# Two attention layers and two expert layers in one kernel: the shared stretch issued in traced order, later stages in small pieces

## The chip, the cores and the metric

The kernel runs on one core of one Trainium2 chip. The metric is the device time of one execution in microseconds; the time shown is the median of three runs. All arithmetic named here is fp32 unless a type is given.

The engines are named as in the profile: PE does matmuls (its weight loads, PEld, overlap them), DVE and ACT work on 128 partitions of vectors, POOL here adds the two halves of a rope and issues gathers, SP issues the other transfers. Each engine has its own queue of instructions[...].

## The reference, cut to what matters

The input is 2048 tokens of 128 channels. Two layers, each an attention and an expert network, every part with a layernorm before it and a residual after it:

```python
x = x + attn0(ln(x))     # 16 heads of 64, all 2048 x 2048 scores, softmax, rope on q and k,
                         # q, k and v from latents of 64
x = x + ffn0(ln(x))      # 16 experts, 4 a token out of the best 2 of 4 groups of experts:
                         # y += (silu(x@W1+b1) * (x@W3+b3)) @ W2 * weight
x = x + attn1(ln(x))     # 8 heads, sparse: I = sum_h idx_w[h] * relu(q_i[h] . k_i)
                         # local 64 keys kept, later keys masked, top 96 of I taken,
                         # their latents gathered, softmax over the 96, weighted sum
x = x + ffn1(ln(x))      # shared expert of width 256, and 2 of 8 experts of width 128 by the
                         # token's position: exact gelu
```

`attn0` needs all keys before any token's output. After it, a token's way through `ffn0` is its own; `attn1` reads the tokens before it; `ffn1` is its own again.

## The kernel before, in words

The kernel is one class, `Program`. `prologue` loads the weights and computes the latents and the tables. `run` then goes through the first attention in 32 **units**: unit u is a pair of heads `pr` (8 of them) and a group `g` of 512 queries (4 of them), all eight pairs of group 0 first. A unit takes four **steps** s, and a step has two **halves**. Three things are under way in every half, for units that lie some steps apart:

- `by_query` (L265 to L282), for unit u: the scores of 128 queries by 512 keys, for both heads: matmuls into two banks `pa` (L275), the negated maximum `mx` on DVE (L280), and `junk` on ACT (L282), an exponential of which only the row sum is kept. This yields maximum and sum of the softmax.
- `by_key` (L316 to L329), for the unit five steps behind (`BEHIND`): the scores again, transposed, into two banks `pb` (L323), the maxima added by a bf16 matmul with `onesb` (L325), and the exponential `e` on ACT (L329).
- `mean` (L331 to L343), one step later: `e` times the latents `ckv` into `po` (L338). After sixteen of them `o<-po` (L343) takes the result out: once a unit.

Once a unit come `rope` (L235; DVE products `t_q` at L254, their sum `q` on POOL at L255; the keys' `kst` go to DRAM as `kd`), `close` (the sums and the maxima), `turn` (L305, transposes of the maxima, evicted as `mrow`) and `project` (L347, the output product `pp`, added to `xr` on DVE). `keys_of` (L263) loads `ka` and `kb` for the step after next from `kd`.

PSUM is cut into a pool `ps` of five banks (`pa`, `pb`, `rope`), one bank for `po`, and a pool `px` of two banks, from which `x()` gives one to everything else, `turn` and `project` included.

**The later stages.** When a group's eight units are through, `follow(g)` starts: a generator that runs `experts0`, `attention1` and `experts1` for its 512 tokens. Each traces a portion of instructions and then yields an estimate of its microseconds. In the halves of the next group's units `advance(us)` pulls such portions until it has spent `us` times `PACE[g]`: after each `by_key` (1.0), after each `by_query` (1.0) and after the two `mean` (2.0), 6 us of pace a half. If a stream isn't at its end when the next begins, its rest is traced at once. Group 3 has no units after it but the last drain steps, so nearly all of its stream is traced after the loop.

- `experts0` (L518): layernorm, the gate with its ranks (`below`), then for each of 16 experts `hidden` (`p1` and `p3` matmuls, `th` and `z` on ACT, `h` on DVE) and, one expert behind, `py` and its four additions to `xr`. Expert weights `wx` are loaded two ahead.
- `attention1` (L634): keys and index keys of the group, then for each tile n of 128 tokens `index_scores` (L701, matmuls `pi`, `rl` on ACT, sums `v` on DVE), `choose` (L733, four rounds of maximum, index and replacement over `v`, whose length grows with n; then `ixT`), 32 gathers `kv<-table` (L756, indirect transfers that POOL issues), `queries` (L772) and, one tile behind, `attend` (L813: rotation `rgc`/`rgs` of the gathered keys, transposes `ptr`, scores `pl`, `mx`, `e`, transposes `pte`, `po1`, `pj`). The order is index_scores(n), choose(n), attend(n-1), queries(n). `pay` issues one gather or more at each yield, while there are any.
- `experts1` (L925): layernorm, ten expert weights `wd`, two shared experts, the eight by position, the sum and the store of the output.

**The order on the queues.** The program is traced in the order above, and then a scheduler orders each engine's queue: it gives each instruction a priority by its place in the trace, moved ahead by `URGENT` = 500 for those within `high_priority`, and lets an instruction pass earlier ones that can't run yet. `keep_in_program_order` pins the gathers and the first two operations of a rotation. The tile framework puts in the semaphores in either case.

Of the kernel before, what the change touches and what calls it, by code (L numbers as in the profile page):

```python
# [16 lines left out]
P = 128  # L17
# [20 lines left out]
URGENT = 500  # L38
PACE = (1.0, 1.1, 1.2, 1.2)
# [24 lines left out]
def layernorm(nc, pool, src, dst, tag):  # L64

    nt = src.shape[1]
    st = pool.tile([P, nt, 6], F32, tag=tag + "st", name=tag + "st")
    mv = pool.tile([P, nt, 2], F32, tag=tag + "mv", name=tag + "mv")
    for n in range(nt):
        nc.vector.bn_stats(st[:, n, :], src[:, n, :])  # L70
        nc.vector.bn_aggr(mv[:, n, :], st[:, n, :])
    v = pool.tile([P, nt], F32, tag=tag + "v", name=tag + "v")
    nc.vector.tensor_scalar(v, mv[:, :, 1], EPS, None, ALU.add)
    r = rsqrt(nc, pool, v, tag)
    for n in range(nt):
        nc.vector.tensor_scalar(
            dst[:, n, :], src[:, n, :], mv[:, n, 0:1], r[:, n : n + 1], ALU.subtract, ALU.mult
        )


def softplus(nc, pool, out, src, one, tag):

    a = pool.tile(list(out.shape), F32, tag=tag + "a", name=tag + "a", bufs=1)
    nc.scalar.activation(a, src, AF.Abs)
    nc.scalar.activation(a, a, AF.Exp, scale=-1.0)
    nc.scalar.activation(a, a, AF.Ln, bias=one)
    nc.vector.scalar_tensor_tensor(out, src, 0.0, a, ALU.max, ALU.add)


def rotate(nc, eng, pool, out1, out2, mu, cos, sin, tag, bufs=None, keep=None):  # L90

    shape = list(mu.shape)
    c = pool.tile(shape, F32, tag=tag + "c", name=tag + "c", bufs=bufs)
    s = pool.tile(shape, F32, tag=tag + "s", name=tag + "s", bufs=bufs)
    first = eng.tensor_tensor(c, mu, bcast(cos, 2, 2), ALU.mult)
    if keep is not None:
        keep(first)
    second = eng.tensor_tensor(s, mu, bcast(sin, 2, 2), ALU.mult)
    if keep is not None:
        keep(second)  # L100
    eng.tensor_tensor(out1, c[:, :, 0, :], s[:, :, 1, :], ALU.subtract)
    eng.tensor_tensor(out2, s[:, :, 0, :], c[:, :, 1, :], ALU.add)


class Program:
# [23 lines left out]
    def bank(self, name):  # L129

        return self.ps_s.tile([P, 512], F32, tag="ps", name=name)
# [5 lines left out]
    def transposed(self, src, dst, name):  # L137

        pt = self.x(name)
        for j in range(4):  # L140
            self.nc.tensor.transpose(pt[:, j, :], src[:, j, :], self.ident)
        self.nc.scalar.copy(dst, pt.rearrange("p a b -> p (a b)"))

    def prologue(self):
# [40 lines left out]
        for g in range(4):  # L187
            cols = slice(512 * g, 512 * g + 512)
            xn = pp.tile([P, 4, C], F32, tag="xn", name=f"xn{g}", bufs=2)
            layernorm(nc, pp, self.xr[g], xn, "ln0")  # L190
            nc.gpsimd.tensor_tensor(self.xr[g], self.xr[g], xn, ALU.add)
            hn = pp.tile([P, 4, C], F32, tag="hn", name=f"hn{g}", bufs=2)
            layernorm(nc, pp, xn, hn, "ln0")
# [33 lines left out]
        self.ep = self.ctx.enter_context(tc.tile_pool(name="a_e", bufs=7))  # L227
# [37 lines left out]
    def by_query(self, u, i):  # L265
# [11 lines left out]
        with self.tc.high_priority(URGENT):  # L277
            for h in range(2):
                at = (slice(None), qt, kc, slice(h, h + 1))
                nc.vector.tensor_reduce(mx[at], ps[h], axis=AX.X, op=ALU.max, negate=True)  # L280
                junk = self.am.tile([P, 512], BF16, tag="junk", name=f"junk{u}_{i}_{h}")
                nc.scalar.activation(junk, ps[h], AF.Exp, bias=mx[at], accum_out=su[at])  # L282
# [22 lines left out]
    def turn(self, u):  # L305

        nc = self.nc
        pm = self.x(f"pt{u}", dtype=BF16)
# [7 lines left out]
    def by_key(self, u, kb):  # L316
# [10 lines left out]
        with self.tc.high_priority(URGENT):  # L327
            for h in range(2):
                nc.scalar.activation(e[:, h, :], ps[h], AF.Exp)  # L329
# [17 lines left out]
    def project(self, u, h):  # L347
# [4 lines left out]
        pm = self.x(f"pp{u}_{h}")  # L352
# [8 lines left out]
    def run(self):  # L361
# [26 lines left out]
        for s in range(4 * NU + BEHIND + 5):  # L388
            u, j = divmod(s, 4)
            ub, jb = divmod(s - BEHIND, 4)  # L390
            um, jm = divmod(s - BEHIND - 1, 4)
            if u < NU and j == 0 and u + 1 < NU:
                self.rope(self.UNITS[u + 1][0], "q", self.UNITS[u + 1][1])
            if u + 1 < 8:
                self.rope(u + 1, "k", j)
            if s == 4 * 8:
                self.keys.close()
            if s + 2 < 4 * NU:
                self.keys_of((s + 2) // 4, (s + 2) % 4, "a")
            sb = s + 2 - BEHIND  # L400
            if 0 <= sb < 4 * NU:
                self.keys_of(sb // 4, sb % 4, "b")
            for half in range(2):
                pair = range(2 * half, 2 * half + 2)
                for i in pair:
                    if 0 <= ub < NU:
                        self.by_key(ub, 4 * jb + i)
                    advance(1.0)
                    if u < NU:
                        self.by_query(u, 4 * j + i)  # L410
                    advance(1.0)
                if half == 1 and u < NU and j == 3:
                    self.close(u)
                for i in pair:
                    if 0 <= um < NU:
                        self.mean(um, 4 * jm + i)
                if half == 0 and j == 0 and 0 <= u - 1 < NU:
                    self.turn(u - 1)
                advance(2.0)
                if jm == 1 and 0 <= um - 1 < NU:  # L420
                    self.project(um - 1, half)
            if jm == 1 and 0 <= um - 1 < NU:
                self.outs.pop(um - 1)
                if um % 8 == 0:
                    if stream is not None:
                        for _ in stream:
                            pass
                    stream, owed, pace = self.follow(um // 8 - 1), 0.0, PACE[um // 8 - 1]
        if stream is not None:
            for _ in stream:  # L430
                pass
# [86 lines left out]
    def experts0(self, sc, g):  # L518
# [6 lines left out]
        layernorm(nc, sm, xr, xn, "ln1")  # L525
        yield 5.0
        xT = sm.tile([P, 512], F32, tag="xT", name=f"xT1_{g}")
        self.transposed(xn, xT, f"pt1_{g}")
        yield 2.0
# [4 lines left out]
        for j in range(4):  # L534
            nc.tensor.matmul(pg[:, j, :], xT[:, j * P : j * P + P], w["wg"], start=True, stop=True)
        s = sm.tile([P, 4, NE0], F32, tag="s", name=f"gs{g}")
# [4 lines left out]
        yield 2.0  # L541
# [3 lines left out]
        def below(v, n, first, k, tag):  # L545
# [3 lines left out]
            eq = sm.tile(shape, F32, tag="eq", name=f"eq{tag}{g}")  # L549
            nc.vector.tensor_tensor(gt, bcast(v, 2, n), bcast(v, 3, n), ALU.is_gt)  # L550
            nc.vector.tensor_tensor(eq, bcast(v, 2, n), bcast(v, 3, n), ALU.is_equal)
            ff = bcast(first.rearrange("p a b -> p (a b)"), 1, 4)
            e2 = eq.rearrange("p t a b -> p t (a b)")
            nc.vector.tensor_tensor(e2, e2, ff, ALU.mult)
            nc.vector.tensor_tensor(gt, gt, eq, ALU.add)
            rank = sm.tile([P, 4, n], F32, tag="rank" + tag, name=f"rank{tag}{g}")
            nc.vector.tensor_reduce(rank, gt, axis=AX.X, op=ALU.add)
            nc.vector.tensor_scalar(rank, rank, float(k) - 0.5, None, ALU.is_lt)
            return rank
# [4 lines left out]
        gsel = below(gm, NG0, w["first4"], 2, "g")  # L564
        yield 3.0
# [6 lines left out]
        esel = below(ms, NE0, w["first16"], 4, "e")  # L572
        yield 7.0
# [13 lines left out]
        yield 2.0  # L587

        pt = self.x(f"ptw{g}", [P, P])
        nc.tensor.transpose(pt, we.rearrange("p a b -> p (a b)"), self.ident)  # L590
        wt = sm.tile([P, P], F32, tag="wt", name=f"wt{g}")
        nc.scalar.copy(wt, pt)
        yield 1.0
        pb = self.x(f"pb2_{g}")
        nc.tensor.matmul(pb.rearrange("p a b -> p (a b)"), wt, w["b2"], start=True, stop=True)
        nc.vector.tensor_tensor(xr, xr, pb, ALU.add)
        yield 1.5


        hs = {}  # L600
        for e in range(NE0 + 1):
            if e < NE0:
                if e + 2 < NE0:
                    wx.append(self.weights(wp, e + 2, f"wb{g}_{e + 2}"))
                hs[e] = self.hidden(hp, wx[e], xT, w["b13"][:, 0, e : e + 1], self.hb[:, e : e + 1], w["b13"][:, 1, e : e + 1], f"b{g}_{e}")
                yield 2.0
            if e > 0:
                h = hs.pop(e - 1)
                py = self.x(f"py{g}_{e}")
                for j in range(4):  # L610
                    nc.tensor.matmul(py[:, j, :], h[:, j * P : j * P + P], wx[e - 1][:, 2, :], start=True, stop=True)
                yield 1.0
                for j in range(4):
                    nc.vector.scalar_tensor_tensor(
                        xr[:, j, :], py[:, j, :], wh[:, j, e - 1 : e], xr[:, j, :], ALU.mult, ALU.add
                    )
                yield 1.0

    def hidden(self, pool, wx, xT, b1, hb1, b3, name):

        nc = self.nc
        p1, p3 = self.x("p1" + name, [P, 512]), self.x("p3" + name, [P, 512])
        nc.tensor.matmul(p1, wx[:, 0, :], xT, start=True, stop=True)  # L623
        nc.tensor.matmul(p3, wx[:, 1, :], xT, start=True, stop=True)  # L624
# [4 lines left out]
        h = pool.tile([P, 512], F32, tag="h", name="h" + name)  # L629
# [486 lines left out]
```

## Time and profile before

| | us |
|---|---|
| Median of the runs shown (3) | 3028.55 |
| Lowest and highest of them | 3015.8 and 3028.8 |
| Profiled execution | 3467.66 |
| Its span, first to last instruction | 3465.9 |
| Busy in it: PE / ACT / DVE / POOL | 2798.2 / 1739.4 / 1715.1 / 577.9 |
| Last `o<-po` (end of the 32nd unit) | 2900.0 |
| Mean granted PE clock | 0.861 |

The profiled execution is 14.5% longer than the median; durations in the text come from it. A matmul's end is modelled in it, so a busy PE need not be a PE at its peak. The 24 units that share their time with later stages lie between 595 and 2900 us, the stages of group 3 between 2900 and 3466.

### The profile page before, as it was taken

Reading aid. Unit: us, or ns where it says so; the run is one execution under the profiler, and the core shown is the slowest. Engines: PE = TensorE matmul, PEld = TensorE weight load, DVE = VectorE, ACT = ScalarE, POOL = GpSimd, SP = SyncE. Lnnn points to the kernel's source line nnn. Section 1 sums busy time; section 2 is a strip of 40 time slices with the busy share of each in tenths; the row PEclk is TensorE's granted clock in tenths of the full one; section 3 lists DMA queues with packets and bytes.
Section 4 is the critical chain, followed back from the end, with each engine's and each line's share of the span. In section 5 each row is a group of like instructions: output and inputs, shape, how many; then the busy total and the mean of one; then the engine's idle time right before and its main releaser. Section 6 shows DMA issues by size and latency. Waiting matters only on the chain. (4 is left out here: it accounts for less than half of the span.)

```text
span 3465.9 us, 38526 instructions
## 1 busy us (share of the span) xinstructions
PE 2798.2 (81%) x13452; PEld 1256.3 (36%) x13452; DVE 1715.1 (49%) x3749; ACT 1739.4 (50%) x4157; POOL 577.9 (17%) x586
## 2 busy tenths in 40 slices
PE   5999999998788899997697899997696877733426
PEld 3444444343233344442243344342242333312214
DVE  7645444565343444665363545555354624664242
ACT  2766667565464566564464466564363542312213
POOL 1111100002313210002312300002303210061330
PEclk7999999999797799998897899997797978856556
DMA  4211111111111111111111111111111101010000
GB/s 130 64 52 52 59 49 38 37 45 33 34 37 27 31 52 38 41 39 28 32 39 28 30 49 43 39 35 28 31 29 25 23 12 42 24 21 5 14 12 26
DMA packets 98097, 127.74 MB, mean 37 GB/s; under 512 B 31344, under 2 KB 49776, under 8 KB 97904
## 3 DMA queue, kind: packets, MB, share of 16 engines
q1 hardware_dynamic: 81520, 108.48, 11.1%
q0 software_dynamic: 16384, 16.81, 2.4%
q8 instruction: 106, 1.74, 0.2%
q14 instruction: 87, 0.71, 0.1%
HBM read 115.26 MB, written 9.96 MB: 36 GB/s over the span
## 5 line engine op out<-in xcount | busy, mean ns | idle before, releaser
L280 DVE TENSOR_REDUCE mx<-pa 128x1 f32<-128x512 f32 x1024 | 673.2, 686 | 695.7 <-PE pa L275 502.3
L282 ACT ACTIVATE junk<-pa,mx 128x512 bf16<-128x512 f32 x1024 | 699.9, 691 | 423.2 <-DVE mx L280 384.5
L275 PE MATMUL pa<-ka,q 64*128 64x512 f32 x2048 | 777.8, 639 | 87.7 <-ACT junk L282 68.2
L329 ACT ACTIVATE e<-pb 128x512 f32<-128x512 f32 x1024 | 556.5, 597 | 473.2 <-PE pb L325 356.2
L323 PE MATMUL pb<-q,kb 64*128 64x512 f32 x2048 | 693.4, 646 | 99.6 <-ACT e L329 73.1
L756 POOL DMA_INDIRECT kv<-table,ixT x512 | 491.0, 959 | 926.1 <-issue 484.2
L338 PE MATMUL po<-e,ckv 128*64 128x512 f32 x2048 | 552.0, 659 | 1.7 <-issue 1.7
L275 PEld LDWEIGHTS pa<-ka,q 64*128 64x128 f32 x2048 | 272.5, 193 | 351.7 <-ACT junk L282 190.3
L323 PEld LDWEIGHTS pb<-q,kb 64*128 64x128 f32 x2048 | 233.7, 193 | 350.9 <-issue 165.6
L255 POOL TENSOR_TENSOR q<-t_q 128x512 f32<-128x512 f32 x32 | 40.7, 1273 | 1560.7 <-DVE t_q L254 1560.7
L325 PE MATMUL pb<-mrow,onesb 64*128 64x512 bf16 x1024 | 262.8, 386 | 2.0 <-issue 1.9
L338 PEld LDWEIGHTS po<-e,ckv 128*64 128x64 f32 x2048 | 133.9, 146 | 348.9 <-issue 337.3
L282 ACT ACTIVATION_READ_ACCUMULATOR junk<-pa,mx 128x1 f32 x1024 | 209.2, 204 | 0.0
L861 DVE TENSOR_REDUCE mx<-pl 128x2 f32<-128x416 f32 x64 | 37.8, 591 | 343.7 <-remote 158.0
L865 ACT ACTIVATE e<-pl,mx 128x208 f32<-128x208 f32 x128 | 54.4, 431 | 242.6 <-DVE mx L862 173.7
L711 PE MATMUL pi<-kiT,qiT 64*128 64x512 f32 (+4 forms) x320 | 123.9, 632 | 47.3 <-issue 17.9
L831 PE MATMUL ptr<-ident,kv 128*128 128x128 f32 x256 | 44.3, 315 | 94.7 <-issue 66.9
L855 PE MATMUL pl<-kr,qT 64*32 64x128 f32 x1024 | 66.9, 320 | 63.6 <-issue 63.5
L325 PEld LDWEIGHTS <-onesb 64*128 64x128 bf16 x1024 | 75.6, 96 | 112.2 <-issue 90.3
L717 DVE SCALAR_TENSOR_TENSOR v<-rl,iw_sb,v 128x512 f32<-128x512 f32 (+4 forms) x120 | 77.1, 644 | 71.9 <-ACT rl L716 64.2
L832 ACT COPY kr<-ptr 128x512 f32<-128x512 f32 x64 | 37.0, 590 | 142.7 <-PE ptr L831 97.0
L630 DVE SCALAR_TENSOR_TENSOR hb<-thb,zb 128x512 f32<-128x512 f32 x64 | 44.3, 692 | 129.4 <-ACT zb L628 127.4
(266 smaller groups left out, 2856.4 us busy)
## 6 DMA issues: line engine op xcount, KB each, us to landing
ka<-kd SPq DMA_DIRECT2D x128, 256.0 KB
kb<-kd SPq DMA_DIRECT2D x128, 256.0 KB
wb<-in_wx SPq DMA_DIRECT2D x64, 192.0 KB
kd<-kst SPq DMA_DIRECT2D x32, 256.0 KB
kv<-table,ixT POOLq DMA_INDIRECT x512
wd<-in_wx SPq DMA_DIRECT2D x40, 192.0 KB
csk<-in_cs SPq DMA_DIRECT2D x4, 512.0 KB
csq<-in_cs SPq DMA_DIRECT2D x4, 512.0 KB
```

What stands on the lines that cost most here:

```text
L275: nc.tensor.matmul(ps[h], q[rows, qt * P : qt * P + P], k[rows, :], start=True, stop=True)
L280: nc.vector.tensor_reduce(mx[at], ps[h], axis=AX.X, op=ALU.max, negate=True)
L282: nc.scalar.activation(junk, ps[h], AF.Exp, bias=mx[at], accum_out=su[at])
L323: nc.tensor.matmul(ps[h], k[rows, c], q[rows, :], start=True, stop=False)
L325: nc.tensor.matmul(ps[h], self.onesb[rows, :], mrow[rows, :], start=False, stop=True)
L329: nc.scalar.activation(e[:, h, :], ps[h], AF.Exp)
L338: nc.tensor.matmul(self.pos[u][cols, :], self.ckv[:, kb, :], e[:, h, :], start=(kb == 0), stop=(kb == NT - 1))
L711: nc.tensor.matmul(pi[:, : hi - lo], qiT[h // 2][rows, q], kiT[rows, lo:hi], start=True, stop=True)
L717: nc.vector.scalar_tensor_tensor(v[:, lo:hi], rl[:, : hi - lo], w["iw"][:, h : h + 1], v[:, lo:hi], ALU.mult, ALU.add)
L756: nc.gpsimd.indirect_dma_start(out=kv[:, 2 * (g % 16) + g // 16, :], out_offset=None, in_=table[0 : P * (n + 1), :], in_offset=bass.Indire ...
L855: nc.tensor.matmul(pl[32 * j : 32 * j + 32, c, 80:NK], qs[rows, 32 * gr : 32 * gr + 32], kr[rows, gr % 16, :], start=False, stop=(c == 1),)
L865: nc.scalar.activation(e[:, i, :], pl[:, c, :], AF.Exp, scale=SCALE1, bias=mx[:, i : i + 1], accum_out=su[:, i : i + 1],)
```

## The change

Four things are changed.

1. The loop of `run` stands inside `tc.manual_schedule()`: there the scheduler leaves each engine's instructions in traced order, on every queue. `URGENT`, its two `high_priority` blocks and the pins of gathers and rotations are gone; the pin of the table preload stays for group 3, whose stream is traced after the loop and is still ordered by the scheduler.
2. The stages are cut into small pieces, about one engine's portion of a chain each, some 450 a group. `layernorm`, `softplus`, `rotate`, `transposed`, `hidden` and `index_scores` become generators. `merge` alternates pieces of choose(n) with pieces of attend(n-1), which came one after the other before. `paced` issues one gather a piece, in `queries`, the next `index_scores` and in what remains after it; during `attend` there are none. An expert's order is now `p1`, then `th` and `z` with `py` of the expert before, then `p3` with the additions of the expert before, then `h` twice.
3. `advance` runs after each of the two `mean` (1.0 each) instead of once after both (2.0). `PACE` is smaller, as are the estimates in the yields.
4. `turn` and `project` take their banks from `ps` instead of `px`; the pool of `e` has eight buffers instead of seven, and `rl` three instead of two. `e*ri` is done in two halves, and the two Gelus of `experts1` stand together.

The number and size of matmuls, transfers and gathers stay as they are. The diff, cut to its core:

```diff
-URGENT = 500
-PACE = (1.0, 1.1, 1.2, 1.2)
+PACE = (0.86, 0.93, 1.0, 1.0)
...
+def merge(*parts):
+    parts = list(parts)
+    while parts:
+        for p in list(parts):
+            us = next(p, None)
+            if us is None:
+                parts.remove(p)
+            else:
+                yield us
...
-        self.ep = self.ctx.enter_context(tc.tile_pool(name="a_e", bufs=7))
+        self.ep = self.ctx.enter_context(tc.tile_pool(name="a_e", bufs=8))
...
-        with self.tc.high_priority(URGENT):
-            for h in range(2):
+        for h in range(2):
...
-        pm = self.x(f"pt{u}", dtype=BF16)
+        pm = self.bank(f"pt{u}", [P, 4, P], BF16)
...
-        pm = self.x(f"pp{u}_{h}")
+        pm = self.bank(f"pp{u}_{h}", [P, 4, C])
...
-        for s in range(4 * NU + BEHIND + 5):
+        with self.tc.manual_schedule():
+            for s in range(4 * NU + BEHIND + 5):
...
                     for i in pair:
                         if 0 <= um < NU:
                             self.mean(um, 4 * jm + i)
-                if half == 0 and j == 0 and 0 <= u - 1 < NU:
-                    self.turn(u - 1)
-                advance(2.0)
+                        advance(1.0)
+                    if half == 0 and j == 0 and 0 <= u - 1 < NU:
+                        self.turn(u - 1)
...
-        def pay(us):
-
-            for _ in range(min(len(gathers), max(1, round(us / 1.8)))):
-                gathers.pop(0)()
-            return us
+        def paced(pieces):
+
+            for us in pieces:
+                if gathers:
+                    gathers.pop(0)()
+                yield us
...
-        pending = None
+        last = iter(())
         for n in range(4 * g, 4 * g + 4):
-            yield from index_scores(n)
+            yield from paced(index_scores(n))
             while gathers:
-                yield pay(1.8)
-            yield from choose(n)
-            if pending is not None:
-                yield from attend(*pending)
-            yield from queries(n)
-            pending = (n, self.kv, self.cl, *self.qT)
+                yield from paced(iter((0.8,)))
+            yield from merge(choose(n), last)
+            yield from paced(queries(n))
+            last = attend(n, self.kv, self.cl, *self.qT)
         while gathers:
-            yield pay(1.8)
-        yield from attend(*pending)
+            yield from paced(iter((0.8,)))
+        yield from last
```

How a portion is cut, for the transposes and for an expert:

```diff
         for j in range(4):
             self.nc.tensor.transpose(pt[:, j, :], src[:, j, :], self.ident)
+        yield 0.8
         self.nc.scalar.copy(dst, pt.rearrange("p a b -> p (a b)"))
+        yield 0.8
...
         nc.tensor.matmul(p1, wx[:, 0, :], xT, start=True, stop=True)
-        nc.tensor.matmul(p3, wx[:, 1, :], xT, start=True, stop=True)
+        yield
...
         nc.scalar.activation(z, p1, AF.Identity, bias=b1)
-        h = pool.tile([P, 512], F32, tag="h", name="h" + name)
+        yield
+        p3 = self.x("p3" + name, [P, 512])
+        nc.tensor.matmul(p3, wx[:, 1, :], xT, start=True, stop=True)
+        yield
         nc.vector.scalar_tensor_tensor(h, th, 1.0, z, ALU.add, ALU.mult)
+        yield
         nc.vector.scalar_tensor_tensor(h, p3, b3, h, ALU.add, ALU.mult)
```

## The prediction

> **What bounds the kernel now.** The page comes first: which engine is busy, and where.
>
> ```profile
> span 3465.9 us, 38526 instructions
> PE 2798.2 (81%) x13452; PEld 1256.3 (36%) x13452; DVE 1715.1 (49%) x3749; ACT 1739.4 (50%) x4157; POOL 577.9 (17%) x586
> ...
> POOL 1111100002313210002312300002303210061330
> PEclk7999999999797799998897899997797978856556
> ```
>
> PE leads with 81%, but its clock dips where POOL's digits rise, so that busy share is partly a stretched one. The row of `o<-po` (L343, one instruction a unit) says where units end; the windows view then cuts the span there. Its columns are length, busy time (count) of PE, PEld, DVE, ACT, POOL, clock, DMA share, GB/s.
>
> ```profile
> L343 ACT COPY o<-po x32: 576/586/601, 181.1 to 2900.0; 128x512 f32<-128x512 f32 x32
> ```
>
> ```profile
> 481.00:538.00 57.00, 57.00 (x252) 23.95 (x248) 26.31 (x51) 40.27 (x101) 1.27 (x1) 1.00 0.14 38
> ...
> 595.00:1360.00 765.00, 678.76 (x3319) 292.61 (x3318) 358.92 (x844) 434.01 (x1045) 133.13 (x136) 0.89 0.14 37
> 1360.00:2115.00 755.00, 647.50 (x3223) 284.12 (x3222) 379.73 (x843) 420.76 (x1006) 133.18 (x136) 0.90 0.14 36
> 2115.00:2900.00 785.00, 649.01 (x3175) 282.45 (x3169) 383.47 (x802) 393.46 (x934) 128.80 (x133) 0.88 0.12 29
> 2900.00:3466.00 566.00, 263.54 (x1383) 152.24 (x1383) 259.93 (x485) 121.94 (x261) 122.61 (x128) 0.63 0.08 19
> ```
>
> A unit alone takes 57 us. With pieces of later stages in it, the 24 units from 595 to 2900 take 2305 us: 96 each, or 12.0 us a half-step (192 halves). The last group's later stages stand alone after 2900: 566 us. ACT has 1248 us of work in the 2305 and DVE 1122, so neither is full. Looking inside with ten short windows where POOL issues gathers:
>
> ```profile
> 912.00:937.00 25.00, 5.88 (x9) 1.64 (x8) 0.69 (x1) 1.97 (x4) 15.76 (x17) 0.54 0.11 24
> ...
> 1678.00:1702.00 24.00, 0.36 (x3) 0.06 (x2) 0.00 (x0) 0.60 (x1) 14.87 (x16) 0.50 0.11 23
> ...
> 2469.00:2491.00 22.00, 0.15 (x1) 0.00 (x0) 0.00 (x0) 0.00 (x0) 13.12 (x14) 0.62 0.11 22
> ...
> sum 263.00, PE 72.70 PEld 32.30 DVE 4.23 ACT 16.12 POOL 177.56; mean PE 7.27 PEld 3.23 DVE 0.42 ACT 1.61 POOL 17.76
> ```
>
> DVE works 4 us in 263: everything stands while POOL issues. Right after one of them (938 to 956) PE is busy 18.00 of 18. Eight lie in the stretch (199 us), two in the tail (64). The POOL timeline shows how dense a burst is:
>
> ```profile
> 890.86 1.26 POOL L255 TENSOR_TENSOR q<-t_q 128x512 f32<-128x512 f32 x1 [41.68 <-DVE t_q L254]
> 892.27 0.96 POOL L756 DMA_INDIRECT kv<-table,ixT  x1
> 893.53 0.95 POOL L756 DMA_INDIRECT kv<-table,ixT  x1 [0.30 <-issue]
> ```
>
> One gather each 1.25 us, 32 a tile: 40 us. No semaphore explains the dead PE; I come back to that.
>
> [...] ACT idled 384.5 us ahead of `junk` waiting for its own `mx`, with other work due behind it. So the order matters, and a piece queued too early blocks what follows. [...]
>
> **The change, part by part.** Durations are of the profiled execution, 3467.66 us (span 3465.9 and 1.8 outside). The median of the runs is 3028.55, 0.873 of it; sums are made in profiled time and multiplied by 0.873.
>
> *Instructions.* Nearly the same: 16 more DVE multiplies, as each `e*ri` is halved (estimate 1 us in all, beside PE). The table preload stays one a group: nothing. Loads, stores and gathers are the same in number and size.
>
> *Fixed order, one piece a slot.* Softmax operations no longer jump ahead by priority; each half has six attention steps (two `pb`, two `pa`, two `po`) with a piece after each. Without pieces I checked the method on this half, as it is already in that order:
>
> ```profile
> 544.97 1.13 PE L323 MATMUL pb<-q,kb 64*128 64x512 f32 x4
> ...
> 546.14 1.02 PE L275 MATMUL pa<-ka,q 64*128 64x512 f32 x4
> ...
> 547.20 1.29 DVE L280 TENSOR_REDUCE mx<-pa 128x1 f32<-128x512 f32 x2 [3.30 <-PE pa L275]
> ...
> 549.33 1.08 ACT L329 ACTIVATE e<-pb 128x512 f32<-128x512 f32 x2
> 549.87 1.94 PE L338 MATMUL po<-e,ckv 128*64 128x512 f32 x8
> ```
>
> Starting each instruction at the later of its queue's previous end and its operands (five `ps` banks in turn), a unit comes to 54.6 us against 57 measured: all walked times get a factor 1.045. With pieces put in, a half in which each slot holds one link of PE→ACT→PE or PE→ACT→DVE (transposes then copy; an expert's p1, `th`/`z`, p3) walks to 11.5 us, one with DVE-only pieces (`choose`) to 8.5. PE's own matmuls in the former are about 8.3 us (5.6 attention, 2.7 transposes), so some 3 us are hops. Six slots a half at 1 us of pace and PACE 0.86, 0.93, 1.0 place the groups' piece costs (my sum of the yields: 313, 339, 368 us in about 450 to 463 pieces) within 330, 357, 384: each stream ends inside its eight units. By group, walked:
> - group 0: experts0 14 halves, 160 us; attention1 43 halves at 9.9, 427; experts1 42; three halves without pieces, 22: 651
> - group 1: 150 + 447 + 39 + 20 = 656
> - group 2: 149 + 500 + 40 + 16 = 705 (wider `choose` and scores)
>
> Sum 2012, times 1.045 = **2102** without burst stalls. Before, 2305 − 199 = 2106 without them. So fixed order by itself I price at nothing: the hops it exposes are paid by the finer cut. If the finer cut hid nothing, see the rival.
>
> *Bursts.* `pay` issued a gather or more at every piece, between `choose` and the end of `queries`; afterwards one a piece, only in `queries`, `index_scores` and the drain, not in `attend`. On POOL they still wait only for `ixT`, so they still run 1.25 us apart, and the `q` additions (1.26 us) stand between them in traced order. The stall's cause isn't shown, so both bounds: 0 to 199 us of it stay. I take half, 100: stretch 2202, **−103**.
>
> *Project and turn on the `ps` banks.* Two `pp` and one `pt` a unit now take a bank in the ring of five. Next `pb` waits for a bank until the four `xr` additions end (four of some 0.3 us, twice a unit): in the walk already. `e` buffers 7→8, `rl` 2→3: bound 0 to −10, taken as 0.
>
> *Loads.* SP's queue is fixed too: `ka`/`kb` loads are two steps ahead (40 us against a few), and stand behind `kd` stores (first eight units, waiting some 4 us for POOL), `wx`, `cl`, `wd` (which waits for attention1's pools). Cover: the two steps; bound 0 to +20, taken 0. Units 0 to 7: 0 to +12, taken 0.
>
> *Tail.* It is outside the manual order. Before, `choose` of tiles 13, 14, 15 is 11 DVE operations of 1.95, 2.09, 2.22 us: 69 us with PE and ACT idle, and `attend` begins only at its end (3211.28). `merge` alternates them. DVE's share of `attend` (some 15 us a tile) remains in line, so I take **−60**; −100 if a burst stall goes too, 0 if the scheduler keeps `choose` first.
>
> Sum: 3466 − 103 − 60 = 3303, with 1.8 outside 3305; times 0.873: **2886 us**.
>
> **Rivals.**
> - *Stalls exist only under the profiler.* For: no semaphore ends them, and the execution is 438 us longer than the median.[...] Then before without them is 3466 − 263 = 3203 us for 3028 timed (0.946) and only the tail gains: 57 us, **2972**. Chance 0.18.
> - *Fixed order makes each half a chain* (other side). One late link, a stream copy ahead of `e`, or `mx` behind a 2 us `choose` operation, holds all queues[...]. For: ACT waits on `mx` already, 348 times. Then all 192 halves take the chain's 11.5 × 1.045 = 12.1: 2323, plus 100 of stalls: +118; with −60 of the tail +58, 3524 + 1.8, **3080**; with all the stalls about 3166. It decides when the mean half of the stretch, stalls included, passes 12.3 us (2365 ÷ 192); mine is 11.5. Chance 0.27.
> - *It does nothing.* Program order already was the priority, so the order hardly changes: **3028**. Against: the priorities of 500 and three pins are gone. Chance 0.10.
>
> **How the numbers follow.** My case has 0.45. One half per cent, 15 us, is about what a measurement of this kernel can tell from no change. Faster: 0.45 + 0.18 = 0.63; same 0.10; slower 0.27. Low end: stalls all gone and −100 in the tail, 3466 − 203 − 100 = 3163, 2764 timed; 2740 for buffers and hops. High end: between the slow case at 3080 and its worst, 3110. My case's own range is 2740 to 2975.
>
> **What would show it.** Right: `o<-po` last at 2750 to 2850 instead of 2900; groups of 650 to 770 us; each group's `out` store before its eighth unit ends; tail near 500 with `attend` transposes between `max` operations. Stalls: windows with DVE at zero during L756, in sum 100 us; if they are as long as before, half of my gain is gone. Wrong: mean half above 12.3, ACT's idle time before `junk` <- `mx` above 384.5, a new wait on `ka`, `kb` or `wd`, or POOL's `q` late so that `pa` of the next unit waits.

## The result and the profile after

The changed kernel takes **3162.86 us** (median of four runs, 3158.39 to 3169.45) where the kernel before takes 3026.03 (now four runs): **1.046** of it, with an interval of 1.0428 to 1.0492. It is slower by 137 us; 2886 was forecast, with 2740 to 3110 as the limits. Chips differ for this kernel, and without that no number below can be read: on two of the five chips used for the experiments the kernel before took 3021 to 3024 us (the first sort below), on the other three 3431 to 3454 (the second sort). No chip of the experiments was seen twice, so whether this belongs to the chip or to its condition at the time is open. The runs of 3026.03 are of the first sort; the profile of before, 3467.66, is like the second.

The page after:

```profile
span 3167.6 us, 38398 instructions
PE 2708.8 (86%) x13452; PEld 1199.8 (38%) x13452; DVE 1705.0 (54%) x3765; ACT 1720.7 (54%) x4153; POOL 583.0 (18%) x586
...
POOL 1100100000252130000432130000441230025232
PEclk8999999999999999999999999899999998875556
```

The profiled execution (3169.45 us) is as long as the median. POOL still has its bursts, but in the shared stretch the clock no longer dips under them: by group it was 0.95 to 0.96, against 0.88 to 0.90 in the profile of before. **Dead windows**, some 20 us in which PE, ACT and DVE hardly work while POOL issues gathers, are missing there; two stretches of the tail that look like them (2844 to 2863 and 3077 to 3100) are waits of DVE for gathers, shown further down. Its units and groups, from the row of `o<-po` and the windows view (length, then busy time and count of PE, PEld, DVE, ACT, POOL; clock, DMA share, GB/s):

```profile
L367 ACT COPY o<-po x32: 565/585/614, 179.4 to 2677.3; 128x512 f32<-128x512 f32 x32
```

```profile
120.00:595.00 475.00, 475.00 (x2069) 200.72 (x2067) 237.79 (x446) 324.05 (x801) 37.88 (x30) 1.00 0.17 50
...
595.00:1290.00 695.00, 639.51 (x3277) 273.60 (x3275) 354.19 (x844) 420.52 (x1028) 133.16 (x136) 0.96 0.14 40
1290.00:1985.00 695.00, 639.37 (x3265) 270.95 (x3263) 381.88 (x852) 419.60 (x1022) 133.81 (x136) 0.95 0.15 40
1985.00:2677.00 692.00, 612.86 (x3115) 257.56 (x3111) 379.71 (x805) 384.98 (x923) 131.52 (x133) 0.95 0.13 35
2677.00:3168.00 491.00, 258.94 (x1437) 153.16 (x1435) 256.16 (x490) 124.69 (x264) 124.37 (x128) 0.65 0.08 21
```

Against the profile of before this looks like a gain of 298 us. But a profile of one sort of chip must not be laid against a time of the other. The stretch of 24 units took 2082 us by these windows (2084 between the ends of its `o<-po`); what it took before on a chip of this sort is the first thing the experiments had to find. And the three longest waits on work of the attention itself, in the waits view (total us, times, longest):

```profile
DVE mx L305 <- PE pa L301: 775.2, 458, 9.3
ACT e L353 <- PE pb L350: 480.2, 257, 8.5
ACT junk L307 <- DVE mx L305: 408.7, 344, 17.6
```

`mx` waited 502.3 us for `pa` in the profile of before, and 487.9 in one without dead windows (the version without later stages of group 3, below). Now it is 775.2: DVE stands longer and waits for PE. DVE is busy for 54% of the span, so I read no price from this alone; it says that PE delivers later.

### The profile page after: what moved, and what is told of

Read it like the earlier page. It is cut to its first block, busy times and chain, and to the rows that moved or that the text cites. A ratio compares the mean times of both kernels' runs of the same rounds, so it can differ in the third digit from the quotient of the medians.

```text
span 3167.6 us, 38398 instructions
## 1 busy us (share of the span) xinstructions
PE 2708.8 (86%) x13452; PEld 1199.8 (38%) x13452; DVE 1705.0 (54%) x3765; ACT 1720.7 (54%) x4153; POOL 583.0 (18%) x586
## 5 line engine op out<-in xcount | busy, mean ns | idle before, releaser
L305 DVE TENSOR_REDUCE mx<-pa 128x1 f32<-128x512 f32 x1024 | 667.4, 687 | 778.6 <-PE pa L301 775.2
L301 PE MATMUL pa<-ka,q 64*128 64x512 f32 x2048 | 712.9, 626 | 36.5 <-ACT junk L307 23.2
L348 PE MATMUL pb<-q,kb 64*128 64x512 f32 x2048 | 624.0, 640 | 0.2 <-DVE xr L381 0.2
L301 PEld LDWEIGHTS pa<-ka,q 64*128 64x128 f32 x2048 | 252.5, 190 | 290.6 <-ACT junk L307 127.4
L348 PEld LDWEIGHTS pb<-q,kb 64*128 64x128 f32 x2048 | 214.8, 191 | 232.9 <-issue 126.7
L350 PE MATMUL pb<-mrow,onesb 64*128 64x512 bf16 x1024 | 240.5, 382 | 0.0
L381 DVE SCALAR_TENSOR_TENSOR xr<-pp,rs,xr 128x128 f32<-128x128 f32 x256 | 71.8, 344 | 85.9 <-PE pp L378 84.6
L866 PE MATMUL ptq<-ident,qq 128*128 128x128 f32 x256 | 48.0, 330 | 68.2 <-ACT qq L859 54.9
L758 ACT ACTIVATE rl<-pi 128x512 f32<-128x512 f32 (+4 forms) x120 | 57.8, 517 | 74.2 <-PE pi L753 61.9
L636 DVE SCALAR_TENSOR_TENSOR xr<-py,wh,xr 128x128 f32<-128x128 f32 x256 | 71.8, 344 | 45.0 <-PE py L633 45.0
L753 PEld LDWEIGHTS pi<-kiT,qiT 64*128 64x128 f32 x320 | 46.2, 206 | 129.2 <-ACT rl L758 58.0
```

What stands on the lines that cost most here:

```text
L301: nc.tensor.matmul(ps[h], q[rows, qt * P : qt * P + P], k[rows, :], start=True, stop=True)
L348: nc.tensor.matmul(ps[h], k[rows, c], q[rows, :], start=True, stop=False)
L350: nc.tensor.matmul(ps[h], self.onesb[rows, :], mrow[rows, :], start=False, stop=True)
L381: nc.vector.scalar_tensor_tensor(xr[:, j, :], pm[:, j, :], self.rs[u][:, j, h : h + 1], xr[:, j, :], ALU.mult, ALU.add)
L636: nc.vector.scalar_tensor_tensor(xr[:, j, :], py[:, j, :], wh[:, j, e : e + 1], xr[:, j, :], ALU.mult, ALU.add)
L753: nc.tensor.matmul(pi, qiT[h // 2][rows, q], kiT[rows, lo:hi], start=True, stop=True)
```

## The experiments

**Theory 1**: a fixed order costs, as what stands on a queue behind a late instruction waits with it (in the changed kernel a maximum whose input was done at 2844.4 us ran at 2863.7, behind `rgc`; more on it below). **Theory 2**: the small pieces cost. The first four versions ran on a chip where the kernel before took 3023.7 us: one of the two changes each way, and both kernels without the later stages of group 3.

*Small pieces, old ordering.*

```diff
-        with self.tc.manual_schedule():
+        with ExitStack():
```

with URGENT on `mx`, `junk` and `e`, and the pins of the gathers and of the table preload put back.

> The new small pieces, merge, PACE and banks, but the old ordering: no manual schedule, the scheduler with URGENT on the softmax operations and the pins of gathers and table preload back. Theory 1 (the fixed order costs[...]): the cost goes away, 2960 to 3040 us. Theory 2 (the cut itself costs, by its lower PACE, more hops and one gather a piece): it stays, 3130 to 3190 us.

Measured: 3353.99 us, ratio 1.1097 (1.106 to 1.1133). Neither theory had that. The waits suggest what it is:

```profile
ACT junk L309 <- DVE mx L307: 649.4, 347, 24.5
...
DVE rgc L104 <- DMA kv<-table,ixT: 420.0, 32, 24.8
```

The scheduler queued `attend`'s rotation on DVE ahead of its gathers' landing: `rgc` waited for them 32 times, up to 24.8 us, and what stood behind it on DVE, `mx` with it, waited too, `junk` then 649.4 us for `mx`. In the profile of before it was 20.0 us in all. The pin of `rgc` is not among those put back. The run therefore tests pieces, `merge` and a free rotation together, and doesn't say what small pieces cost.

*Old portions, traced order.*

```diff
+        man.enter_context(self.tc.manual_schedule())
...
-        ... name="a_e", bufs=7
+        ... name="a_e", bufs=8
...
-        pm = self.x(f"pt{u}", dtype=BF16)
+        pm = self.bank(f"pt{u}", [P, 4, P], BF16)
```

`URGENT` goes too, as do the pins in the shared stretch; group 3 keeps them.

> The old pieces, PACE and choose-then-attend, but in traced order on every queue. For that order not to wait in a circle it has the eighth e buffer, project and turn on the ps banks and a second h tile in experts1. Theory 1: portions of several hops in a fixed order are worse than small ones, 3250 to 3500 us. Theory 2: close to the kernel before, 3000 to 3060 us.

Measured: 3084.5 us, 1.0193 (1.0165 to 1.0222). Fixed order costs 61 us with the old portions, more than theory 2 and less than theory 1 had it; so the rest of the change costs another 78. The banks and buffers belong to the order and are part of the 61: `e5` of a half needs the buffer that a `mean` traced after it sets free, and `project` could take the second `px` bank while the first waits for a piece traced later. The scheduler can order them otherwise; traced order would, by my reading of the kernel, wait in a circle. No run shows it.

*Without the later stages of group 3* (both kernels; the edit leaves them out).

```diff
     def follow(self, g):
+        if g == 3:
+            self.nc.sync.dma_start(<rows of group g of out>, self.xr[g])
+            return
```

> The kernel before without the later stages of group 3: its rows of the output are the first attention's result. That leaves the prologue and the 32 units with the streams of groups 0 to 2. From the profile of before the tail would be 566 us; if only the profiled execution has the burst stalls, about 490 to 500 in a timed run. Theory 1: 2520 to 2560 us, so that the units take far less than the 2900 of the profile. If the profile's excess lies evenly over the span: 2900 x 0.873 = 2532 as well, so this run by itself does not tell where it lies, its own profile does.

> The changed kernel without the later stages of group 3, as for the kernel before. Its profile is as long as its timed run, so 2675 to 2695 us. Theory 1 (the loss is in the shared stretch): 130 to 170 us more than the kernel before cut likewise. Rival (the loss is in the tail, by merge or the last pieces): the two cut kernels within 30 us of each other.

Measured: 2561.8 and 2693.33 us, 131.5 apart. So the tail costs 462 before (3023.7 − 2561.8) and 470 after (3162.86 − 2693.33, two sets of runs, so less sure): **the loss is in the shared stretch, and the forecast gain of the tail isn't there.** Their windows over the 24 units, before and after:

```profile
592.90:2547.50 1954.60, 1850.67 (x9709) 820.41 (x9709) 1121.60 (x2489) 1241.17 (x2981) 395.84 (x405) 0.97 0.15 40
```

```profile
593.90:2671.00 2077.10, 1887.48 (x9658) 801.02 (x9658) 1115.64 (x2500) 1225.55 (x2974) 398.29 (x405) 0.96 0.14 38
```

With the scheduler's order PE is busy 1851 of 1955 us; in traced order 1887 of 2077. PE's idle time goes from 104 to 190 us, and its busy time grows by 37. The undisturbed stretch before is 1955 us, not 2305.

**Theory 3**: the alternation of `choose` and `attend` is what the small pieces lose. The first versions for it ran on a chip where the kernel before took 3431.3 us.

```diff
-            yield from merge(choose(n), last)
+            yield from choose(n)
+            yield from paced(last)
```

> The changed kernel, traced order and small pieces, but choose(n) first and then attend(n-1), as before; gathers one a piece, in attend too. Theory 3 (alternating choose and attend is what the small pieces lose: each of attend's links stands behind a 1 to 2 us choose operation on DVE, and gathers start late): attention1 of a group falls from 430-474 to about 395-445 us, the tail from 491 to about 455, 3030 to 3080 us in all. Rival (the small pieces lose in experts0 and everywhere, by one hop a slot): 3130 to 3170 us, attention1 stays.

> The small pieces under the old ordering (scheduler, URGENT, pins) with choose before attend. The merged form stood 420 us with DVE waiting in rgc for gathers, its pinned rotation being issued early. Theory 3: without merge the pinned rotation stands behind choose again, the waits of rgc on gathers fall to under 30 us, 2980 to 3060 us. Rival (pieces too small for the scheduler's priorities, merge or not): above 3200 us.

> The kernel before itself, for a second profile. If the dead windows at gather bursts belong to one profiled execution: span near the median, 3020 to 3035 us, no window of 18 us with DVE at zero, stretch of the 24 units some 1955 us as in its cut form. If they come with every profile of this kernel: 3400 to 3500 us.

> The kernel before with eight e buffers and three rl buffers, nothing else. The prediction bounded this part at 0 to -10 us and took 0: 3010 to 3030 us.

Measured: 3585.42 us, 1.0439 (1.0395 to 1.0483); 3416.64, 0.9959 (0.9939 to 0.9979); 3435.43, one run; 3435.09, 1.0011 (0.9993 to 1.0028). The absolute expectations fell, as this chip is of the other sort. Two things follow. The buffers alone do nothing measurable. And the dead windows come and go with the sort of chip: the kernel before, profiled again here, has them, and its profiled execution is as long as the other runs beside it (3435.43 and a median of 3431.3); on chips of the first sort the profiled executions lack them. So being profiled is not enough to make them. Two of them:

```profile
900.00:927.00 27.00, 4.42 (x20) 1.43 (x16) 0.47 (x1) 1.34 (x4) 18.15 (x20) 0.67 0.15 37
1655.00:1678.00 23.00, 1.58 (x3) 0.29 (x2) 0.16 (x1) 0.78 (x2) 17.21 (x20) 0.54 0.16 37
```

The waits of the profile of before, of the same sort, narrow it:

```profile
ACT e L329 <- remote: 94.4, 11, 25.1
DVE mx L280 <- remote: 65.0, 7, 26.2
```

`remote` says that a semaphore's update ended the wait and that the profile has no instruction that ends near it. In the profile of before there are 45 such waits, 430.8 us in sum. The semaphore is each time one that PE's matmuls update, and the update comes 1.5 to 26.2 us after the last recorded instruction of PE that updates it. All seven kept profiles with a time of the second sort have 40 to 48 such waits, 235 to 551 us in sum; of all the others only one has any, a single one of 7.5 us. So ACT and DVE do wait on a semaphore in the dead windows, for PE. What holds PE there is not shown.

`rgc` waited 300.3 us for gathers in the small pieces without merge under the scheduler, 22 times: that expectation (under 30 us) fell too, the rotation being unpinned here as well. Yet this version lost nothing, so the 420 us further up are no price by themselves: here such waits may have stood where the engines stood anyway. It is the only version with gathers that measured below the kernel before, by 0.4%, and it was tried on this sort of chip only.

On another chip of the second sort (3451.88 us for the kernel before): the changed kernel, again without `merge`, and both kernels with one plain transfer for a tile's 32 gathers. That transfer takes the table's first 128 rows and leaves the selected ones out.

```diff
-            gathers.extend(gather(g) for g in range(32))
+            nc.sync.dma_start(kv, bcast(table[0:P, :], 1, 32))
```

> The changed kernel itself. The kernel before took 3024 us on one chip and 3431 on another, with dead windows at gather bursts in the profile of the second. On a chip of the first sort: 3150 to 3175 us, 1.045 of before. On one of the second sort, if the changed kernel's gathers stall too: 3500 to 3600, about 1.03 to 1.05 of before; if its later and thinner gathers don't: 3170, faster than before there.

> The changed kernel with choose before attend, again, beside the changed kernel on the same chip. Theory 3 (the alternation is what the small pieces lose in fixed order): 60 to 130 us less than the changed kernel. Rival (one hop a slot everywhere): within 30 us of it.

> The kernel before with the 32 indirect gathers of a tile replaced by one plain transfer of the same size from the table's first 128 rows, issued by SP (the selected rows are left out). If the gathers' bursts are what stops the engines on some chips: 2980 to 3030 us on any chip. If something else of such a chip is slow: the time stays near the kernel before there.

> The changed kernel with the same replacement. Theory 1 and 3 (fixed order and alternation cost in PE, ACT and DVE, not in gathers): 110 to 150 us over the kernel before without gathers, on any chip. Rival (the changed kernel loses by late gathers, whose rgc waits were 102 us): within 50 us of it.

Measured: 3579.51 us, 1.0352 (1.0306 to 1.0399); 3590.64, 1.0389 (1.0347 to 1.0432); **3009.43**; **3093.58**. Without `merge` the changed kernel is no faster, against theory 3. On this chip the gathers cost 442 us before and 486 after; on the other sort the kernel before with gathers (3021 to 3024) is within 15 us of this one without. So the gathers, as POOL issues them, are what stops the engines on some chips, and the change does not help there. Without gathers the two kernels differ by 84 us, between the two expectations. Windows for stretch and tail, first before, then after:

```profile
593.90:2548.20 1954.30, 1856.04 (x9713) 822.21 (x9713) 1115.81 (x2491) 1245.10 (x2985) 31.95 (x21) 0.97 0.16 41
2548.20:3006.90 458.70, 253.08 (x1379) 147.50 (x1379) 258.63 (x482) 121.06 (x260) 0.00 (x0) 0.66 0.09 21
```

```profile
603.90:2710.70 2106.80, 1907.78 (x9713) 812.89 (x9713) 1117.22 (x2503) 1230.43 (x2978) 29.35 (x21) 0.95 0.15 38
2710.70:3099.50 388.80, 245.81 (x1379) 143.83 (x1379) 252.96 (x487) 122.05 (x261) 0.00 (x0) 0.69 0.11 27
```

The stretch is 152 us longer, the tail **70 shorter**: the gain of the tail exists where no gather is waited for. 58 of the 70 lie in `attention1`. With gathers it is taken back; the waits of the changed kernel between 2677 and 3168 are large enough for that:

```profile
DVE rgc L103 <- DMA kv<-table,ixT: 87.5, 8, 23.0
```

The next versions ran on a chip with 3021.29 us, most of them without gathers. Such kernels should be alike on every chip: the stretch before was 1954 us without gathers on a chip of the second sort, and 1955 with them on one of the first. But no version without gathers was run on two chips, so what is compared across chips below rests on that.

*No merge.* Edit as above.

> The changed kernel without gathers (one plain transfer of 128 fixed rows in their place) and with choose before attend. Base: 3094 us with merge, of which the tail 399. Theory 3 (alternation costs the stretch 30 to 40 us a group): stretch 2085 to about 1990, tail longer by some 57, 3040 to 3070 us. Rival (alternation costs nothing there): only the tail's 57 us come on top, 3140 to 3160 us.

Measured: 3128.73 us (3111.23 to 3136.14). The profiled execution of 3111 has a stretch of 2127 us and a tail of 389. That is between the two expectations. Theory 3 falls: without alternation the stretch is not shorter, and the tail is the same 389, so it isn't `merge` that shortens the tail either.

*Three slots of 2.0 in place of six of 1.0.*

```diff
                         if 0 <= ub < NU:
                             self.by_key(ub, 4 * jb + i)
-                        advance(1.0)
                         if u < NU:
                             self.by_query(u, 4 * j + i)
-                        advance(1.0)
+                        advance(2.0)
...
-                        advance(1.0)
+                    advance(2.0)
```

> The changed kernel without gathers, with three slots of 2.0 in a half (after each by_key/by_query pair and after both means) in place of six of 1.0. Theory 4 (one hop a slot: PE stands in each slot for the link before it): two consecutive links in one slot change places with the attention's steps, 2085 of the stretch falls by 30 to 50 us, 3040 to 3065 us. Rival (the slots don't matter, or pairs are worse as both links wait in place): 3090 us or more.

Measured: 3153.37 us, a stretch of 2171. Theory 4, that each slot costs PE the wait for one link, falls as well: three slots with two links each are worse.

*Old portions in traced order, without gathers.*

> The old portions in traced order, without gathers. Base: the kernel before without gathers, 3009 us. With gathers this order cost 61 us. Theory 1 (fixed order itself costs 60 to 80 us in the stretch, the cut the rest): 3060 to 3090 us. Rival (fixed order costs only through gathers that are issued elsewhere): within 15 us of 3009.

Measured: 3071.64 us. Theory 1 holds at its lower end: 62 us over the 3009.43 of the other chip. The windows show all of it in the stretch, as idle time of PE (98 to 165 us), and nothing in the tail:

```profile
604.10:2620.20 2016.10, 1851.18 (x9713) 821.07 (x9713) 1126.26 (x2491) 1241.82 (x2985) 26.59 (x21) 0.96 0.16 40
2620.20:3072.70 452.50, 248.65 (x1379) 144.75 (x1379) 259.00 (x483) 120.98 (x260) 0.00 (x0) 0.66 0.09 21
```

*The tail alone, under the old ordering, with gathers*: for group 3 `choose(n)` alternates with `queries` and `attend` of tile n−2.

```diff
+                if len(pending) > 1:
+                    yield from merge(choose(n), late(*pending.pop(0)))
```

> The kernel before, changed in the tail alone: for group 3, queries and attend of tile n-2 alternate with choose of tile n (three kv buffers, no pins on the rotation), so that gathers have a whole tile's time to land. Two of four choose phases, 22.9 + 24.4 us, come beside other work: 2980 to 3000 us where the kernel before takes 3024, 30 to 50 less than it on any chip. Rival (the scheduler's order or the waits for gathers take it back): within 10 us of the kernel before.

Measured: 3049.45 us, 1.0097 (1.0066 to 1.0127), 1% slower. `rgc` still waited 71.3 us for gathers in the tail, and two `attend` now stand uncovered at the end.

On a last chip (3454.48 us for the kernel before), again without gathers: the slot between the two means, and the density of the pieces.

```diff
                             self.mean(um, 4 * jm + i)
-                        advance(1.0)
+                    advance(2.0)
```

> The changed kernel without gathers, with one advance of 2.0 after both means as before, in place of 1.0 after each; the four others stay. Theory 5 (the piece between the two means is what the small pieces lose, as it parts PE's longest run of ready matmuls): experts and attention1 halves fall towards the old portions' 11.0 and 10.6 us, 3030 to 3060 us. Rival (it doesn't matter): 3085 to 3105 us. Pairs of pieces were worse in three slots, so above 3105 is open too.

> The changed kernel without gathers, with PACE 1.05, 1.13, 1.2 in place of 0.86, 0.93, 1.0: the same pieces in some 18% fewer halves, more of the halves without any. Theory 6 (a half pays for having pieces at all): attention1 of group 0 in about 29 halves, the stretch shorter by 40 to 70 us, 3030 to 3060 us. Rival (a half pays by its pieces, so that packing gives nothing): 3080 to 3120 us.

Measured: **3043.01** us and 3118.68. Theory 5, that it is the piece between the two means, holds: one slot after both in place of one after each is worth 51 us. Its windows:

```profile
593.90:2653.60 2059.70, 1877.68 (x9713) 818.38 (x9713) 1116.49 (x2503) 1229.76 (x2978) 29.36 (x21) 0.96 0.15 39
2653.60:3041.60 388.00, 245.66 (x1379) 144.02 (x1379) 252.86 (x487) 122.21 (x261) 0.00 (x0) 0.68 0.11 26
```

2060 in the stretch, against 2107 with six slots. PE's busy time makes 30 of these 47 us and its idle time 17. The `po` matmuls in the two stretches, five slots and then six (ends of matmuls are modelled, so the split is rough):

```profile
L362 PE MATMUL po<-e,ckv 128*64 128x512 f32 x1536 | 399.4, 643 | 0.0
```

```profile
L362 PE MATMUL po<-e,ckv 128*64 128x512 f32 x1536 | 420.0, 653 | 0.0
```

So 21 of the 47 us are the broken run of `po` itself. Counted by the `mx<-pa` between `pk` and the last `pj` of group 0, attention1 takes 35 halves of 10.67 us, against 35 of 11.14. Theory 6, that a half pays for having pieces at all, falls: denser pieces cut the halves to 29 and make each 11.98 us.

The stretch without gathers, as the runs add it up:

| version | stretch | PE busy | PE idle | tail | step in the stretch |
|---|---|---|---|---|---|
| before, scheduler's order | 1954 | 1856 | 98 | 459 | |
| old portions, traced order | 2016 | 1851 | 165 | 453 | +62: fixed order, with its banks and buffers |
| small pieces, five slots | 2060 | 1878 | 182 | 388 | +44: the small pieces and what else comes with them |
| small pieces, six slots (the change) | 2107 | 1908 | 199 | 389 | +47: a slot between the means |

The stretch begins at 594 us in two of these profiles and at 604 in the other two; these 10 us are in no row.

With gathers, on chips without dead windows, the shares are others. The stretch is 1955 before, 2037 with the old portions in traced order (595.7 to 2633.0) and 2077 with the change: +82 for the fixed order, +40 for the rest. That the old portions lose only 61 us in all is due to a tail some 14 us shorter. The change's tail and that of the kernel before, difference of times, are 470 and 462. Together with the stretch that is +130, of 137 measured; most of what is missing is the end of the shortened kernels, 7 us after the last `o<-po` before and 16 after.

## Why the prediction was wrong

**The base of the sum failed, and with it the price of the order.** "Before, 2305 − 199 = 2106 without them" is the mis-sized term: undisturbed, the stretch takes 1955 us. The eight windows in it held 199 us; between a chip with the disturbance and one without lie 2276 − 1955 = 321 us, by the second profile of before:

```profile
594.10:2870.20 2276.10, 1951.16 (x9709) 854.22 (x9709) 1121.98 (x2489) 1248.03 (x2981) 393.94 (x405) 0.90 0.13 35
```

Of these 321 us 221 are PE's idle time. The other 100 are the same 9709 matmuls, busy for 1951 us in place of 1851 at a mean clock of 0.90 in place of 0.97; no count of dead windows holds them, though the prediction had called the busy share a stretched one. My walk of the changed order came to 2102 and the change measured 2084, 0.9% off. Some of that is luck: by group it had 680, 686 and 737, and 686, 699 and 699 were measured. Set against 1955 it would have said +147 and the right sign. It was compared with a number that still held 151 us of disturbance, and so "fixed order by itself I price at nothing". The reason that it gave, that the finer cut pays for the hops, did not hold either: fixed order costs 62 us without gathers and 82 with them, and the finer cut comes on top, 91 or 40.

**0.873 was not a scale.** It joined a profile of one sort of chip to times of another; on one chip they agree, within 0.3% in the changed kernel (3169.45 to 3162.86). An evenly spread factor took 12.7% off the changed kernel too, where nothing was to be taken off.

**The bursts.** "I take half": neither. On the chips without dead windows there was nothing to gain; on the others all of it stayed, 442 us before and 486 after.

**The tail.** −60 was of the right size and not the right account: 70 us come without gathers, but with or without `merge`, and with gathers 87.5 us of waits in `rgc` take them back. The prediction had no wait for gathers in the tail, and not that `choose` of the next tile would stand behind `rgc` on DVE. The pins that the change removes are the likely cause of both the gain and the wait; that was not tried alone.

**Not priced at all: where the slot between the means stands.** I counted six slots as given. A piece between the two means costs 47 us of the stretch without gathers; with gathers it was not measured.

**The rivals.** Rival two named the mechanism, chains in a fixed order, and the direction; but its point of decision, a mean half of 12.3 us, stood on the same base. The change is slower at a mean half of 10.9 (2084 ÷ 192), as before it was 10.2. Rival one had the dead windows absent from the timed runs, as they were, but for another reason (they go with the sort of chip), and a gain in the tail alone. "It does nothing" is out.

**Right**: the stages' lengths in group 0 (halves of `experts0` walked 12.0, measured 12.4; of `attention1` 10.3 and 10.45); units 0 to 7 unchanged; buffers at nothing (1.0011); no new wait of note on loads, where the weight load of `pb` waited 1.5 us for `ka`. The first of the forecast signs, `o<-po` last between 2750 and 2850, came out at 2677, earlier than a gain would have asked, with a slower kernel: a sign taken against a disturbed profile says nothing.

**What stands behind a waiting instruction.** On DVE, `rgc` waited 420.0 us for gathers in the small pieces under the old ordering, where `junk` waited 649.4 us for `mx` (384.5 in the profile of before), and 87.5 us in the tail of the changed kernel. There one `v` was done at 2844.4 us, and the maximum over it, which stood behind `rgc`, ran only at 2863.7. On ACT, in the profile of before, the scores of one `e` were done at 648.0 us; the `junk` ahead of it waited for `mx` until 650.5, and `e` ran at 651.8.

**Open**: what holds PE on some chips while POOL issues gathers; why the small pieces in five slots still cost 44 us, 27 of them as busy time of PE; where the 26 us come from that the slot between the means costs beyond the longer `po`; why the shares are others with gathers. The new order with five slots and pinned rotations in the tail was not tried with gathers.

## What to carry to other kernels

Before a profile's time is scaled to a median, lay the two executions' times side by side. Here they differed by 14.5% and the profile showed another condition (2305 us for the stretch that takes 1955 undisturbed), so the sum had to be made on an undisturbed stretch, such as a cut version's. Where a scheduler keeps PE busy for 95% of a stretch, as here, a new order has little idle time to win (104 us) and more to lose: it has to be walked instruction by instruction and set against that, not against the old total. And an instruction that waits for a transfer belongs on its queue only behind the work that covers it: in the tail `rgc` waited 87.5 us for gathers, and ready work with it.

## What was not expected of the hardware

- The same kernel takes 3021 to 3024 us on some chips and 3431 to 3454 on others, and all of the difference goes when 512 indirect gathers become 16 plain transfers (3009.43 on a chip of the second sort, where it was 3451.88). In the dead windows shown here and in the prediction, 22 to 27 us each, DVE works under 1 us and PE 0.2 to 6 us at a granted clock of 0.50 to 0.67, while POOL issues one gather each 1.25 us, as it does in the profile of the changed kernel on the first sort.
- In one fixed order, parting two runs of four `po` matmuls by a piece costs 47 us in 192 halves, 0.24 us a half; 21 of the 47 are longer busy time of these matmuls.
